# First attention: the scores of two heads computed together, with the high-times-high products in separate halves of the array's rows

## The chip, the cores and the metric

The kernel runs on one core of one Trainium2 chip, as one launch. The metric is the device time of that launch in microseconds. The time of a kernel is given as the median of several runs, and one further execution is recorded by the hardware profiler; its views (a page, groups of instructions by line, waits, the chain of waits, the order of time, sums by stretch) are what the text below reads. TensorE is called PE, its weight loads PEld, VectorE DVE, ScalarE ACT, GpSimd POOL and SyncE SP.

## The reference, cut to what matters

The program is a network of several layers on a sequence of 1024 positions of 256 values: a causal attention, a feed-forward part that selects positions, a second attention, the feed-forward part again, and a last layer with a recurrence. Only the first attention is touched:

```python
B, S, HID = (1, 256, 256)      # the hidden states that are given have S = 1024
H, KVH, HD = (32, 8, 64)
q = (hidden_states @ Wq.T).reshape(b, s, H, HD).transpose(0, 2, 1, 3)
k = (hidden_states @ Wk.T).reshape(b, s, KVH, HD).transpose(0, 2, 1, 3)
v = (hidden_states @ Wv.T).reshape(b, s, KVH, HD).transpose(0, 2, 1, 3)
...
q = apply_rope(q)
k = apply_rope(k)
k = jnp.repeat(k, groups, axis=1)          # groups = 4
v = jnp.repeat(v, groups, axis=1)
logits = jnp.einsum('bhqd,bhkd->bhqk', q, k) * scale
logits = jnp.where(causal, logits, jnp.finfo(dtype).min)
attn = jax.nn.softmax(logits, axis=-1)
out = jnp.einsum('bhqk,bhkd->bhqd', attn, v)
out = out.transpose(0, 2, 1, 3).reshape(b, s, H * HD)
return out @ Wo.T
```

So there are eight groups of four query heads that share one key head and one value head, of 64 values each, and a query sees the keys up to its own position.

## The kernel before

Positions are handled in eight tiles of 128 (`t` from 0 to 7), heads in eight groups (`g`, with `HG = 4` query heads each). A value is kept as two numbers of a format with fewer bits (F32R): a high part, which is the rounded value, and a low part, which is the rest. A product of two such values is the sum of up to four products of parts.

For each group and tile, `project` (L345 and after) multiplies by the weights, applies the rotation in DVE (L360 to L369), and makes the high and low parts of the four query heads and the one key head: a cast on ACT (L373) writes the high parts, and two subtractions write the low parts (the first group on DVE, all later ones on POOL, through the helper `pair`, L216). In the tile `qk` they lie as low, high for each head. `flip` transposes them on PE (L385 for queries, L392 for keys) and copies the results to `qs` and `ks` (ACT, L389 and L396). After that a head's low part is in rows 0 to 63 and its high part in rows 64 to 127 of `qs[:, h]`; `ks[:, 0]` holds the key as low over high, `ks[:, 1]` as high over low. One matmul over all 128 rows then gives two products of parts at once: with `ks[:, 0]` low times low plus high times high, with `ks[:, 1]` the two mixed ones.

For tile `t` there are `n = (t + 1) * 128` keys. `spans(n)` gives the number `k` of PSUM banks (1 up to 512 columns, otherwise 2) and the columns `w` in each. The scores of a head are made in one of two forms:

- for `t >= 4`, `scores` takes one head: two matmuls for each bank (L409), one more that adds the causal mask to the last 128 columns (L413), and then `softmax`: the maximum on DVE (L298), the exponential with its sum on ACT (L303), the reciprocal on DVE (L306) and the normalisation on POOL (L307);
- for `t < TWO`, with `TWO = 4`, `two_scores` takes two heads: each has one bank of the same tile `s`, with two matmuls and a mask matmul each (L428, L429), one reduce on DVE for both maxima (L430), two exponentials (L433), two reciprocals (L436) and two normalisations (L438).

A tile `s` has two banks, and there are two such tiles; all other matmul results of the stage use four further tiles `b` of one bank. After the scores, `turn` transposes the weights of four heads for one block of 128 keys (L444), `split_pt` makes their high part on ACT (L313) and their low part on DVE (L314), and `mix` multiplies them with the values (L455, L456). `fold` adds the two halves of the result (L466, L470, and POOL by L219 and L216), and `wout` multiplies by the output weights (L224 to L226) and adds to `x` (L484).

The order of the work is set by a list of events with due times, `(time, step)`, which is sorted and then issued. Its unit is one block of 128 keys, and a tile takes `n = t + 1 + GAP` units. The scores of tile `t` are due ahead of its first `turn`, by `LEAD` and a share of `A_LEN * n`; `PH` shifts the pairs. Each engine runs its instructions in the order that the scheduler of the program gives it from these events; an instruction that is ready may be placed between two of another event.

Of the kernel before, what the change touches and what calls it, by code (L numbers as in the profile page):

```python
# [10 lines left out]
F32 = mybir.dt.float32  # L11
# [4 lines left out]
AF = mybir.ActivationFunctionType  # L16
ALU = mybir.AluOpType
AX = mybir.AxisListType
PSUM = bass.MemoryType.PSUM

P = 128
T = 1024
# [11 lines left out]
LEAD = 4.56  # L34
# [21 lines left out]
A_LEN = 0.94  # L56
LAG = 2.22
GAP = 0.79
TWO = 4
PH = 0.62  # L60


def f(ap):
    return ap.bitcast(F32)
# [19 lines left out]
def spans(n):  # L84

    k = (n + 511) // 512
    return k, n // k


class Net:  # L90
# [227 lines left out]
    def attn_a(self):  # L318
        nc, tc = self.nc, self.tc
        G, HG, HD = 8, 4, 64  # L320
        NQ = HG + 1
        with ExitStack() as ctx:
            pool = self.layer_pool(ctx, "aa")
            grp = {}
# [19 lines left out]
            def project(g, t):  # L344
                z = grp[g]  # L345
                o = slice(t * P, t * P + P)
                pq = self.ps("b", bufs=4)
                for c in range(2):
                    self.mm3(
                        pq[:, : NQ * HD + HD], [a[c][:, o] for a in xT],  # L350
                        [a[:, c, :] for a in z["wq"]], c == 0, c == 1,
                    )
                raw = pool.tile([P, NQ + 1, HD], F32, tag="t1", name=self.nm("t1"))
                t2 = pool.tile([P, NQ, HD], F32, tag="t2", name=self.nm("t2"))
                p3 = pq[:, : NQ * HD + HD].rearrange("p (h d) -> p h d", d=HD)
                q3, t1 = p3[:, :NQ, :], raw[:, :NQ, :]
                cb = cos[:, t : t + 1, :].to_broadcast([P, NQ, HD])
                for a in range(2):
                    sb = sin[:, t : t + 1, 32 * a : 32 * a + 32].to_broadcast([P, NQ, 32])
                    nc.vector.tensor_tensor(  # L360
                        t2[:, :, 32 * a : 32 * a + 32], q3[:, :, 32 - 32 * a : 64 - 32 * a],
                        sb, op=ALU.mult,
                    )
                nc.vector.tensor_tensor(t1, q3, cb, op=ALU.mult)
                v = z["v"]
                pv = pq[:, NQ * HD : NQ * HD + HD]
                nc.scalar.copy(v[:, t, 0, :], pv)
                nc.vector.tensor_tensor(v[:, t, 1, :], pv, f(v[:, t, 0, :]), op=ALU.subtract)
                nc.vector.tensor_tensor(t1, t1, t2, op=ALU.add)  # L369

                qk = pool.tile([P, NQ * 2 + 1, HD], F32R, tag="qk", name=self.nm("qk"))
                lo, hi = (qk[:, : NQ * 2, :].rearrange("p (h a) d -> p h a d", a=2)[:, :, a, :] for a in range(2))
                nc.scalar.copy(hi, t1)  # L373
                sub = self.pair if g else nc.vector.tensor_tensor
                sub(lo, t1, f(hi), op=ALU.subtract)
                sub(qk[:, NQ * 2, :], t1[:, HG, :], f(hi[:, HG, :]), op=ALU.subtract)
                z["qh"][t] = qk

            def flip(g, t):
# [17 lines left out]
                    z["ks"][:, :, o], pt[:, : 2 * P].rearrange("p (h q) -> p h q", q=P)  # L397
                )

            def scores(g, t, h, pr):  # L400
                z = grp[g]
                qs, ks = z["qs"], z["ks"]
                o = slice(t * P, t * P + P)
                n = (t + 1) * P
                s = self.ps("s", [P, 2, 512])
                k, w = spans(n)
                for b in range(k):
                    for a in range(2):
                        nc.tensor.matmul(  # L409
                            s[:, b, :w], qs[:, h, o], ks[:, a, b * w : (b + 1) * w],  # L410
                            start=a == 0, stop=a == 1 and b < k - 1,
                        )
                nc.tensor.matmul(s[:, k - 1, w - P : w], self.identb, self.maskb, start=False, stop=True)  # L413
                pr[h] = self.softmax(pool, 8, s[:, :k, :w], n)

            def two_scores(g, t, h0, pr):

                z = grp[g]
                qs, ks = z["qs"], z["ks"]
                o = slice(t * P, t * P + P)  # L420
                n = (t + 1) * P
                s = self.ps("s", [P, 2, 512])
                m, l, r = (
                    self.small.tile([P, 2], F32, tag=k, name=self.nm(k), bufs=6) for k in ("smm", "sml", "smr")
                )
                for i in range(2):
                    for a in range(2):
                        nc.tensor.matmul(s[:, i, :n], qs[:, h0 + i, o], ks[:, a, :n], start=a == 0, stop=False)  # L428
                    nc.tensor.matmul(s[:, i, n - P : n], self.identb, self.maskb, start=False, stop=True)  # L429
                nc.vector.tensor_reduce(m, s[:, :, :n], AX.X, ALU.max, negate=True)  # L430
                pp = [pool.tile([P, 512], F32, tag="p_", name=self.nm("p_"), bufs=8) for _ in range(2)]
                for i in range(2):
                    nc.scalar.activation(  # L433
                        pp[i][:, :n], s[:, i, :n], AF.Exp, bias=m[:, i : i + 1], scale=1.0, accum_out=l[:, i : i + 1]
                    )
                    nc.vector.reciprocal(r[:, i : i + 1], l[:, i : i + 1])  # L436
                for i in range(2):
                    nc.gpsimd.tensor_scalar(pp[i][:, :n], pp[i][:, :n], r[:, i : i + 1], 1.0, op0=ALU.mult, op1=ALU.mult)  # L438
                    pr[h0 + i] = pp[i]

            def turn(g, t, kt, pr, st):
                pt = self.ps("b", bufs=4)
                for h in range(HG):
                    nc.tensor.transpose(  # L444
                        pt[:, h * P : (h + 1) * P], pr[h][:, kt * P : (kt + 1) * P], self.ident,
                    )
                st[kt] = self.split_pt(pt, 512)

            def mix(g, t, kt, st):
                z = grp[g]  # L450
                if kt == 0:
                    st["po"] = self.ps("b", bufs=4)
                hi, lo = st.pop(kt)
                vv = z["v"][:, kt, :, :].rearrange("p a d -> p (a d)")
                nc.tensor.matmul(st["po"], vv, hi, start=kt == 0, stop=False)  # L455
                nc.tensor.matmul(st["po"], vv, lo, start=False, stop=kt == t)  # L456
# [29 lines left out]
            ev, at = [], 0.0  # L486
            for g in range(G):
                g0 = at
                for t in ORD[min(g, 1) + (g == G - 1)]:
                    n = t + 1 + GAP  # L490
                    pr, st = {}, {}
                    if t < TWO:
                        for h in range(0, HG, 2):
                            ev.append((at - LEAD - A_LEN * n + A_LEN * n * (h + PH) / HG, lambda g=g, t=t, h=h, pr=pr: two_scores(g, t, h, pr)))
                    for h in range(HG if t >= TWO else 0):
                        ev.append((at - LEAD - A_LEN * n + A_LEN * n * (h + 0.5) / HG, lambda g=g, t=t, h=h, pr=pr: scores(g, t, h, pr)))
                    for kt in range(t + 1):
                        ev.append((at + kt, lambda g=g, t=t, kt=kt, pr=pr, st=st: turn(g, t, kt, pr, st)))
                        ev.append((at + kt + LAG, lambda g=g, t=t, kt=kt, st=st: mix(g, t, kt, st)))
                    ev.append((at + t + LAG + 0.1, lambda g=g, t=t, st=st: fold(g, t, st)))  # L500
                    ev.append((at + t + LAG + 4, lambda g=g, t=t: wout(g, t)))
                    at += n
                if g + 1 < G:
                    d = at - g0
                    lo, hi = (g0 + w * d for w in ((W0, W1) if g else FIRST))
                    ev.append((lo, lambda g=g + 1: weights(g)))
                    for t in range(NT):
                        ev.append((lo + (hi - lo) * (t + 1) / NT, lambda g=g + 1, t=t: project(g, t)))
                        ev.append((lo + (hi - lo) * (t + 2.2) / NT, lambda g=g + 1, t=t: flip(g, t)))
            for t in range(NT):  # L510
                ev.append((PRO[0] + PRO[1] * t, lambda t=t: project(0, t)))
                ev.append((PRO[0] + PRO[1] * (t + PRO[2]), lambda t=t: flip(0, t)))
# [1152 lines left out]
```

## Time and profile before

| | |
|---|---|
| median of 3 runs | 1554.46 us (1554.23 to 1555.32) |
| the profiled execution | 1553.83 us |
| its span, from the first to the last instruction | 1552.1 us |
| mean granted TensorE clock over the span | 0.956 |
| PE, recorded busy | 1381.5 us (89%) |
| DVE | 1200.5 us (77%) |
| ACT | 945.3 us (61%) |
| POOL | 707.2 us (46%) |

The score matmuls of the first attention (L409, L428) run between about 30 and 630 us of the span. Matmul records have a start that is measured and an end that is modelled, so consecutive matmuls overlap in the records, and the distance between two starts tells what one costs. A group line gives the line, engine, operation, names, shapes and count, then the busy time in us and the mean of one in ns, then the engine's idle time before these instructions and what ended most of it. A line of the order of time gives the start in us, the length in us, the engine, the instruction and how many were merged.

### The profile page before, as it was taken

The page shows a single profiled execution, that of the slowest core. Times are in us where ns is not written, and L with a number is a line of the kernel's source. Part 1 is how long each engine was busy: PE and PEld are TensorE (multiplying, and loading weights), DVE is VectorE, ACT ScalarE, POOL GpSimd, SP SyncE. Part 2 cuts the span into 40 slices and gives each one's busy share as a digit, 9 for nine tenths or more (in the row PEclk, how much of TensorE's full clock was granted, in tenths as well). Part 3 has the DMA queues.
Part 4 walks back from the last instruction along what each step waited for, and adds up shares of the span by engine and source line. Part 5 has one row for each costly group of instructions (what it writes and reads, how often), then busy time and mean ns, then how long its engine had stood idle before and what let it go on. Part 6 is the DMA issues. An engine that isn't in the chain of part 4 may idle for free. (4 is left out here: it accounts for less than half of the span.)

```text
span 1552.1 us, 25113 instructions
## 1 busy us (share of the span) xinstructions
PE 1381.5 (89%) x8626; PEld 1143.4 (74%) x8626; DVE 1200.5 (77%) x2562; ACT 945.3 (61%) x2049; POOL 707.2 (46%) x1059
## 2 busy tenths in 40 slices
PE   5999999999999999677789999999996786986898
PEld 4788888888888888546678788877885464765787
DVE  5888999999998999864667777775774666977657
ACT  4777777777878787622466665665563432555533
POOL 4656666666565654523654534544312322346100
PEclk9999999999999999899899999999998697997999
DMA  3000000000000020330265555555568311000000
GB/s 95 11 8 11 8 11 8 12 8 12 8 1 1 1 82 29 113 109 21 47 119 106 112 113 109 115 101 109 89 138 233 143 58 37 28 21 1 1 1 28
DMA packets 169391, 87.65 MB, mean 56 GB/s; under 512 B 154032, under 2 KB 154288, under 8 KB 166960
## 3 DMA queue, kind: packets, MB, share of 16 engines
q1 hardware_dynamic: 169264, 86.05, 23.0%
q8 instruction: 68, 1.11, 0.3%
q14 instruction: 59, 0.48, 0.1%
HBM read 47.23 MB, written 1.05 MB: 31 GB/s over the span
## 5 line engine op out<-in xcount | busy, mean ns | idle before, releaser
L314 DVE TENSOR_TENSOR pt<-b,pt 128x512 fp32r<-128x512 f32 x288 | 192.8, 684 | 22.4 <-ACT pt L313 18.8
L313 ACT CAST pt<-b 128x512 fp32r<-128x512 f32 x288 | 165.1, 591 | 46.6 <-PE b L444 43.5
L307 POOL TENSOR_SCALAR p<-p,smr 128x640 f32<-128x640 f32 (+3 forms) x128 | 125.5, 980 | 89.9 <-DVE smr L306 82.7
L303 ACT ACTIVATE p<-s,smm 128x640 f32<-128x640 f32 (+3 forms) x128 | 123.2, 963 | 25.9 <-DVE smm L298 21.2
L298 DVE TENSOR_REDUCE smm<-s 128x1 f32<-128x640 f32 (+3 forms) x128 | 129.7, 1013 | 5.6 <-PE s L413 5.2
L409 PE MATMUL s<-ks,qs 128*128 128x320 f32 (+3 forms) x512 | 133.3, 366 | 0.6 <-ACT p L303 0.5
L455 PE MATMUL b<-pt,v 128*128 128x512 f32 x288 | 132.5, 460 | 0.3 <-ACT pt L313 0.3
L444 PE MATMUL b<-ident,p 128*128 128x128 f32 x832 | 122.8, 273 | 0.2 <-ACT qs L389 0.2
L456 PE MATMUL b<-pt,v 128*128 128x512 f32 x288 | 120.6, 419 | 0.1
L444 PEld LDWEIGHTS b<-ident,p 128*128 128x128 f32 x832 | 96.9, 141 | 10.7 <-ACT qs L389 1.8
L409 PEld LDWEIGHTS s<-ks,qs 128*128 128x128 f32 x512 | 89.3, 189 | 13.0 <-ACT p L303 4.2
L734 PE MATMUL b<-ptr,v 128*128 128x256 f16 (+1 forms) x320 | 83.4, 266 | 10.7 <-DMA ptr<-hl 9.4
L678 ACT ACTIVATE p<-s,smm 128x640 f32<-128x640 f32 (+1 forms) x64 | 60.8, 950 | 47.9 <-DVE smm L676 47.7
L216 POOL TENSOR_TENSOR qk<-t,qk 128x320 fp32r<-128x320 f32 x112 | 64.5, 597 | 49.9 <-ACT qk L373 49.9
L667 PE MATMUL s<-qk 128*128 128x320 f32 (+3 forms) x384 | 85.7, 358 | 0.5 <-ACT p L678 0.3
L735 PE MATMUL b<-ptr,v 128*128 128x256 f16 (+1 forms) x320 | 84.8, 265 | 0.0
L716 DVE SCALAR_TENSOR_TENSOR hl<-p,smr,hl 128x640 f16<-128x640 f32 (+1 forms) x64 | 71.7, 1120 | 15.2 <-ACT hl L701 13.6
L736 PE MATMUL b<-ptr,v 128*128 128x256 f16 (+1 forms) x320 | 83.3, 265 | 0.0
L701 ACT ACTIVATE hl<-p,smr 128x640 f16<-128x640 f32 (+1 forms) x64 | 63.2, 988 | 19.8 <-DVE smr L695 11.7
L693 POOL TENSOR_SCALAR p<-p,smr 128x128 f32<-128x128 f32 (+1 forms) x64 | 33.7, 532 | 88.4 <-DVE smr L691 81.5
L428 PE MATMUL s<-ks,qs 128*128 128x256 f32 (+3 forms) x256 | 66.9, 356 | 4.5 <-ACT p__78_391 L433 1.7
L667 PEld LDWEIGHTS s<-qk 128*128 128x128 f32 x384 | 65.4, 188 | 7.5 <-ACT p L678 1.4
(1036 smaller groups left out, 4554.5 us busy)
## 6 DMA issues: line engine op xcount, KB each, us to landing
wqkv<-in_wqkv_f SPq DMA_DIRECT2D x8, 1024.0 KB, 5.9
wof<-in_wo_f SPq DMA_DIRECT2D x4, 1024.0 KB, 6.8
bias<-in_bqkv_f SPq DMA_DIRECT2D x16, 256.0 KB, 3.4
raw<-in_wqk_b SPq DMA_DIRECT2D x16, 256.0 KB, 3.3
wgu<-in_wgu_f SPq DMA_DIRECT2D x4, 1024.0 KB, 6.1
raw<-in_wqkv_a SPq DMA_DIRECT2D x8, 384.0 KB, 3.2
raw<-in_wo_a SPq DMA_DIRECT2D x8, 256.0 KB, 2.7
wd<-in_wd_f SPq DMA_DIRECT2D x2, 1024.0 KB, 4.7
```

The lines of the kernel that those rows point to most:

```text
L298: nc.vector.tensor_reduce(m, s, AX.XY, ALU.max, negate=True)
L303: nc.scalar.activation(p[:, :n].rearrange("p (a b) -> p a b", a=s.shape[1]), s, AF.Exp, bias=m, scale=1.0, accum_out=l)
L307: nc.gpsimd.tensor_scalar(p[:, :n], p[:, :n], r, 1.0, op0=ALU.mult, op1=ALU.mult)
L313: nc.scalar.copy(hi[:, :n], pt[:, :n])
L314: nc.vector.tensor_tensor(lo[:, :n], pt[:, :n], f(hi[:, :n]), op=ALU.subtract)
L409: nc.tensor.matmul(s[:, b, :w], qs[:, h, o], ks[:, a, b * w : (b + 1) * w], start=a == 0, stop=a == 1 and b < k - 1,)
L444: nc.tensor.transpose(pt[:, h * P : (h + 1) * P], pr[h][:, kt * P : (kt + 1) * P], self.ident,)
L455: nc.tensor.matmul(st["po"], vv, hi, start=kt == 0, stop=False)
L456: nc.tensor.matmul(st["po"], vv, lo, start=False, stop=kt == t)
L667: nc.tensor.matmul(s[:, i, :w], z[a][:, o], z[b][:, i * w : (i + 1) * w], start=j == 0, stop=j == 2 and i < k - 1,)
L734: nc.tensor.matmul(d, vh, hi, start=kt + i == 2 * b, stop=False)
L735: nc.tensor.matmul(d, vh, lo, start=False, stop=False)
```

## The change

`scores` and `two_scores` become one function that handles two heads for every tile. The queries of the second head of each pair are stored as high over low, those of the first as low over high. The two mixed products of a head remain one matmul over all rows, with the key copy that fits. Low times low is no longer computed. High times high is a matmul over 64 rows: for the first head rows 64 to 127, for the second rows 0 to 63, each into a bank of its own. All mixed products of the pair come first, then the halves, then the two masks. For `t >= 4` the pair takes both tiles `s`. The maximum is reduced for each head by itself in every tile. The high parts are cast by two instructions on ACT, one for the queries and one for the key, and the low part of the key is written twice by one subtraction. The due times of the tiles with `t >= 4` are now those of pairs.

```diff
--- before.py
+++ after.py
@@ -56,7 +56,6 @@
 A_LEN = 0.94
 LAG = 2.22
 GAP = 0.79
-TWO = 4
 PH = 0.62
 
 
@@ -369,11 +368,14 @@
                 nc.vector.tensor_tensor(t1, t1, t2, op=ALU.add)
 
                 qk = pool.tile([P, NQ * 2 + 1, HD], F32R, tag="qk", name=self.nm("qk"))
-                lo, hi = (qk[:, : NQ * 2, :].rearrange("p (h a) d -> p h a d", a=2)[:, :, a, :] for a in range(2))
-                nc.scalar.copy(hi, t1)
+                q4, tq = qk[:, : 2 * HG, :].rearrange("p (j a) d -> p j a d", a=4), t1[:, :HG, :].rearrange("p (j e) d -> p j e d", e=2)
+                hi, lo = q4[:, :, 1:3, :], q4[:, :, 0:4:3, :]
+                hik, lok = qk[:, 2 * HG + 1 : 2 * HG + 2, :], qk[:, 2 * HG : 2 * HG + 3 : 2, :]
+                nc.scalar.copy(hi, tq)
+                nc.scalar.copy(hik, t1[:, HG:NQ, :])
                 sub = self.pair if g else nc.vector.tensor_tensor
-                sub(lo, t1, f(hi), op=ALU.subtract)
-                sub(qk[:, NQ * 2, :], t1[:, HG, :], f(hi[:, HG, :]), op=ALU.subtract)
+                sub(lo, tq, f(hi), op=ALU.subtract)
+                sub(lok, t1[:, HG:NQ, :].to_broadcast([P, 2, HD]), f(hik).to_broadcast([P, 2, HD]), op=ALU.subtract)
                 z["qh"][t] = qk
 
             def flip(g, t):
@@ -397,46 +399,49 @@
                     z["ks"][:, :, o], pt[:, : 2 * P].rearrange("p (h q) -> p h q", q=P)
                 )
 
-            def scores(g, t, h, pr):
+            def scores(g, t, h0, pr):
+
+
                 z = grp[g]
                 qs, ks = z["qs"], z["ks"]
                 o = slice(t * P, t * P + P)
                 n = (t + 1) * P
-                s = self.ps("s", [P, 2, 512])
                 k, w = spans(n)
+                s = [self.ps("s", [P, 2, 512]) for _ in range(k)]
+                s = [s[i] for i in range(2)] if k == 2 else [s[0][:, i : i + 1, :] for i in range(2)]
+                for i in range(2):
+                    for b in range(k):
+                        nc.tensor.matmul(
+                            s[i][:, b, :w], qs[:, h0 + i, o], ks[:, 1 - i, b * w : (b + 1) * w], start=True, stop=False,
+                        )
                 for b in range(k):
-                    for a in range(2):
+                    for i in range(2):
+                        half = slice(64 * (1 - i), 64 * (1 - i) + 64)
                         nc.tensor.matmul(
-                            s[:, b, :w], qs[:, h, o], ks[:, a, b * w : (b + 1) * w],
-                            start=a == 0, stop=a == 1 and b < k - 1,
+                            s[i][:, b, :w], qs[half, h0 + i, o], ks[half, i, b * w : (b + 1) * w],
+                            start=False, stop=b < k - 1,
                         )
-                nc.tensor.matmul(s[:, k - 1, w - P : w], self.identb, self.maskb, start=False, stop=True)
-                pr[h] = self.softmax(pool, 8, s[:, :k, :w], n)
-
-            def two_scores(g, t, h0, pr):
-
-                z = grp[g]
-                qs, ks = z["qs"], z["ks"]
-                o = slice(t * P, t * P + P)
-                n = (t + 1) * P
-                s = self.ps("s", [P, 2, 512])
+                for i in range(2):
+                    nc.tensor.matmul(s[i][:, k - 1, w - P : w], self.identb, self.maskb, start=False, stop=True)
                 m, l, r = (
-                    self.small.tile([P, 2], F32, tag=k, name=self.nm(k), bufs=6) for k in ("smm", "sml", "smr")
+                    self.small.tile([P, 2], F32, tag=k_, name=self.nm(k_), bufs=6) for k_ in ("smm", "sml", "smr")
                 )
                 for i in range(2):
-                    for a in range(2):
-                        nc.tensor.matmul(s[:, i, :n], qs[:, h0 + i, o], ks[:, a, :n], start=a == 0, stop=False)
-                    nc.tensor.matmul(s[:, i, n - P : n], self.identb, self.maskb, start=False, stop=True)
-                nc.vector.tensor_reduce(m, s[:, :, :n], AX.X, ALU.max, negate=True)
-                pp = [pool.tile([P, 512], F32, tag="p_", name=self.nm("p_"), bufs=8) for _ in range(2)]
+                    c = slice(i, i + 1)
+                    nc.vector.tensor_reduce(m[:, c], s[i][:, :, :w], AX.XY, ALU.max, negate=True)
+                    if n > 512:
+                        p = self.get("P", [P, T], F32, "p")
+                    else:
+                        p = pool.tile([P, 512], F32, tag="p_", name=self.nm("p_"), bufs=8)
+                    nc.scalar.activation(
+                        p[:, :n].rearrange("p (a b) -> p a b", a=k), s[i][:, :, :w], AF.Exp, bias=m[:, c], scale=1.0,
+                        accum_out=l[:, c],
+                    )
+                    nc.vector.reciprocal(r[:, c], l[:, c])
+                    pr[h0 + i] = p
                 for i in range(2):
-                    nc.scalar.activation(
-                        pp[i][:, :n], s[:, i, :n], AF.Exp, bias=m[:, i : i + 1], scale=1.0, accum_out=l[:, i : i + 1]
-                    )
-                    nc.vector.reciprocal(r[:, i : i + 1], l[:, i : i + 1])
-                for i in range(2):
-                    nc.gpsimd.tensor_scalar(pp[i][:, :n], pp[i][:, :n], r[:, i : i + 1], 1.0, op0=ALU.mult, op1=ALU.mult)
-                    pr[h0 + i] = pp[i]
+                    p = pr[h0 + i][:, :n]
+                    nc.gpsimd.tensor_scalar(p, p, r[:, i : i + 1], 1.0, op0=ALU.mult, op1=ALU.mult)
 
             def turn(g, t, kt, pr, st):
                 pt = self.ps("b", bufs=4)
@@ -489,11 +494,8 @@
                 for t in ORD[min(g, 1) + (g == G - 1)]:
                     n = t + 1 + GAP
                     pr, st = {}, {}
-                    if t < TWO:
-                        for h in range(0, HG, 2):
-                            ev.append((at - LEAD - A_LEN * n + A_LEN * n * (h + PH) / HG, lambda g=g, t=t, h=h, pr=pr: two_scores(g, t, h, pr)))
-                    for h in range(HG if t >= TWO else 0):
-                        ev.append((at - LEAD - A_LEN * n + A_LEN * n * (h + 0.5) / HG, lambda g=g, t=t, h=h, pr=pr: scores(g, t, h, pr)))
+                    for h in range(0, HG, 2):
+                        ev.append((at - LEAD - A_LEN * n + A_LEN * n * (h + PH) / HG, lambda g=g, t=t, h=h, pr=pr: scores(g, t, h, pr)))
                     for kt in range(t + 1):
                         ev.append((at + kt, lambda g=g, t=t, kt=kt, pr=pr, st=st: turn(g, t, kt, pr, st)))
                         ev.append((at + kt + LAG, lambda g=g, t=t, kt=kt, st=st: mix(g, t, kt, st)))
```

## The prediction

> **What bounds the kernel now.** First the busy digits of the page, to find the stretch that the change touches, then the sums of that stretch by engine.
>
> ```profile
> PE   5999999999999999677789999999996786986898
> DVE  5888999999998999864667777775774666977657
> ```
> ```profile
> core 0: us, PE busy (x) PEld busy (x) DVE busy (x) ACT busy (x) POOL busy (x), PEclk, DMA share, GB/s
> 60.00:600.00 540.00, 535.19 (x3467) 451.04 (x3467) 489.72 (x1100) 422.84 (x983) 329.15 (x494) 1.00 0.04 14
> ```
>
> The first attention fills slices 2 to 16 (about 40 to 640 us). PE is recorded busy for 535.19 of 540 us, DVE for 489.72, at full clock and with hardly any DMA. The chain that ended last is followed back only to the second half of the span, so it says nothing here; and recorded matmul ends are modelled, so PE must be read by its starts. The order of time of PE alone gives those:
>
> ```profile
> 230.65 0.34 PE L226 MATMUL b<-wh,xT 128*128 128x384 f32 x1
> 230.83 0.33 PE L224 MATMUL b<-wh,xT 128*128 128x384 f32 x1
> 231.00 0.33 PE L225 MATMUL b<-wl,xT 128*128 128x384 f32 x1
> ...
> 232.36 0.44 PE L409 MATMUL s<-ks,qs 128*128 128x384 f32 x1
> 232.64 0.38 PE L392 MATMUL b<-ident,qk 128*128 128x128 f32 x2
> 232.78 0.59 PE L409 MATMUL s<-ks,qs 128*128 128x384 f32 x2
> ...
> 234.76 0.23 PE L413 MATMUL s<-maskb,identb 128*128 128x128 bf16 x1
> 234.80 0.47 PE L455 MATMUL b<-pt,v 128*128 128x512 f32 x1
> 235.12 0.39 PE L456 MATMUL b<-pt,v 128*128 128x512 f32 x1
> 235.34 0.40 PE L455 MATMUL b<-pt,v 128*128 128x512 f32 x1
> 235.58 0.46 PE L409 MATMUL s<-ks,qs 128*128 128x320 f32 x2
> ```
>
> Four things are seen. A 384-column matmul starts 0.17 us after the last, but is recorded with 0.33 to 0.34: some 0.163 us of each is a tail that the next one overlaps. After a mask matmul, which the next follows by 0.04 us, a 512-column matmul costs 0.32 (234.80 to 235.12) where it otherwise costs 0.22 to 0.24: its weight load, recorded at 188 ns, is then not hidden, for about 85 ns. A chain of scores is not kept together: at 232.64 the transposes of L392 stand inside one. And there are few holes. Over all starts from 60 to 600 us I count about 480 to 500 us of such starts' own distances, 33 us of 85 ns load exposures (400 of them) and some 20 us of longer holes. So PE bounds this stretch, with about 4% to spare; DVE comes next with 9% (50 us of 540) idle. What PE gains can be used only until DVE binds, at about half its size; what PE loses is paid nearly in full.
>
> **The change part by part.** Start distances within the chains of L409 are 146, 175, 202 and 231 ns for 320, 384, 448 and 512 columns (t = 4 to 7); 256 columns of L224 to L226 take 118.
>
> Matmuls removed. Per pair of heads and bank, four full products become two full and two half-row ones. If the two halves run beside each other, one start distance goes. Nothing in the trace runs two matmuls at once. Bounds: no gain (halves one after the other), or a whole distance: for t = 0 to 7 109, 118, 175, 231, then twice 146, 175, 202 and 231, 2141 ns; 16 pairs of each t (8 groups by 2), 34.3 us. I take less, since each half has a weight load of its own, and 128-column transposes, whose loads are as many as they, come every 109 ns: two halves then cost the larger of one distance and 220 ns. Saved: 0, 18, 130, 231, 144, 260, 368, 462 = 1613 ns by 16 = **25.8 us**.
>
> Masks. Both masks of a pair now stand at its end: one 85 ns exposure of a following load instead of two, but the second mask's own load (recorded at 96 ns) shows beyond the 38 ns of the first, about 58. Saved 27 ns by 128 pairs = **3.5 us** (0 to 10.9).
>
> Changes of the array's partition. Each pair goes from 128 rows to two halves and back: 256 changes. In the count of starts, 70 of 496 L409 matmuls (14%) have a foreign one next. With three borders inside a pair's halves for t of 4 and more and one below (256 borders), 14% broken adds two changes each, 72: **328 in all**. No matmul of the trace uses fewer than 128 rows, so the price has to be bounded: 0 (nothing is waited for), or the tail and a whole unhidden load, 163 + 188 = 351 ns. Below nothing is excluded, for a change does no work. I take the tail alone, 163 ns, the row nearest to waiting until the array is empty: 328 × 0.163 = **53.5 us**. The weights are loaded ahead everywhere in this trace, so I leave their 188 ns to the range.
> The row first: the 0.163 us tail is overlapped at every start shown, full array after full array. The Trainium skill, "TensorEngine Tiling (Array Packing)", Key Properties, states a rule that speaks against this change: going to another tiling mode, not just another tile, drains the engine. By it each of the 328 changes pays, without it none, and the sum would be 29 us of PE saved; no row here can show which.
> For the overlap of the halves, the nearest row is the 231 ns between 512-column starts. The skill's "TensorE: Matmul & The Clock Gate", Part 3, has row tiles start about 4 ns apart; by that page the saving would be the upper bound of 34.3 us, and it says nothing of tiles that alternate with the full array.
>
> DVE. For t below 4 one reduce of both heads becomes two. From the rows:
>
> ```profile
> L298 DVE TENSOR_REDUCE smm<-s 128x1 f32<-128x1024 f32 x32 | 38.8, 1213 | 1.9 <-PE s L413 1.7
> L298 DVE TENSOR_REDUCE smm<-s 128x1 f32<-128x640 f32 x32 | 26.0, 813 | 0.3 <-PE s L413 0.2
> L430 DVE TENSOR_REDUCE smm<-s 128x2 f32<-128x256 f32 x16 | 6.6, 411 | 0.0
> ```
>
> (1213 − 813) / 384 = 1.042 ns per element, so 146 ns are fixed; 64 more reduces add 9.3 us. DVE's 50 idle us hide it as long as PE binds: 0, and up to 9.3 if not.
>
> ACT and POOL. The 320-column cast of L373 (462 ns) becomes 256 columns (408 by the 128x256 cast of L875) and 64 (222 by L367): +168 ns, 64 times, 10.8 us on an engine with 117 of 540 idle: 0. POOL's two subtractions keep their total (872 + 321 ns against about 736 + 459). Who waits behind:
>
> ```profile
> POOL qk L216 <- ACT qk L373: 49.9, 24, 3.4
> ...
> PEld s L409 <- ACT p L303: 4.0, 16, 0.5
> ```
>
> POOL waits longer for that cast, but PE waited for POOL's result only 1.7 us in all; without that cover 10.8 us. No DMA is added, and nothing moves on SP's queue.
>
> Buffers. For t of 4 and more a pair now takes both score buffers at once, and the next pair's first matmul, with all transposes and mixes queued behind it on PE, waits for the first exponential of this one. Pairs come 0.47 n units apart; 8 groups of 42.3 units in about 595 us make a unit 1.76 us, so 7.3 us for t = 7 and 4.8 for t = 4. The buffer is held for matmuls, two reduces and an exponential, about 1.6 + 2.4 + 1.3 + 0.4 = 5.7 and 1.0 + 1.6 + 1.0 + 0.4 = 4.0 us. It fits: 0, taken from the second row above (4.0 us of waits today); if it does not, about 0.5 us by 64 pairs, 32 us.
>
> Sum on PE: − 25.8 − 3.5 + 53.5 = **+24.2 us**, paid in full. The profiled execution took 1553.83 us (span 1552.1 and 1.7 around it), 0.6 below the median of the runs, so 1553.8 + 24.2 + 0.6 = 1578.6: **1578 us**.
>
> **The rivals.**
> *The changes are cheap* (0 to 50 ns). For it: PE reorders nothing but hides every load here. Against: the tail must go somewhere. PE then saves 29 down to 13 us; half can be used before DVE binds, and the 9.3 us of reduces take some back: 1540 to 1552, say **1545**. It decides below 29.3 / 328 = 89 ns per change: beneath that the kernel is not slower.
> *Load not hidden either*, 351 ns: 328 × 0.351 = 115 − 29 = +86; some changes share their wait, so 250 ns and more, 1607 to 1640, say **1620**. For it: after a mask the load is already exposed by 85 ns.
> *The halves run one after the other*, so the change does not do what it says: 53.5 − 3.5 = +50 us, **1604**. For it: no two matmuls overlap in the trace.
> *The buffers do not suffice*: with the forecast's price +24 + 32, **1610**; with cheap changes + 32 − 10, 1576.
>
> **How the numbers follow.** Forecast (tail alone, 1564 to 1592) 0.32; cheap changes 0.31; load exposed 0.17; halves in turn 0.11; buffers 0.09. The likeliest is 1578. The range goes from 1543, which leaves out the better part of the cheap case (about 0.1), to 1618, which leaves out the dearest load cases (0.1). About 0.2% (3.1 us) is what a measurement can tell from no change. Faster: 0.27, nearly all of the cheap case; same 0.05, from its upper end; slower 0.68.
>
> **What would show it.** Right: half-row score matmuls of which two start closer together than 100 ns, the gap from the last full matmul to the first half at 0.16 us or more beyond its usual distance, and again on the way back to the masks; the stretch of the first attention some 24 us longer, all later stretches the same; DVE's idle share in it higher than 9%. Wrong: starts that follow without a gap at the change (the cheap case), halves a whole distance apart, more than 20 us of PE waiting for ACT at the scores (buffers), or DVE's idle time nearly gone with PE showing holes (DVE the bound).

## The result, and the profile after

The changed kernel takes 1605.77 us (median of 4 runs) where the kernel before takes 1554.89 us in the same series: a ratio of 1.0338, with a 95% interval of 1.0310 to 1.0365. It is slower by 51 us. The forecast was 24 us slower: the direction and the range hold, the size does not. The profiled execution took 1604.71 us, with a span of 1602.8 us.

The busy digits of the page after (PE, then DVE), to be held against those of before: the first attention now reaches about a slice further.

```profile
PE   5999999999999999977589999999897676886898
DVE  6888888888888888876467677767774767887666
```

The sums over the stage, from 20 us to its end, for the kernel before (620 us) and after (676 us). The columns are the stretch, its length, then busy time and number of instructions of PE, PEld, DVE, ACT and POOL, the clock, the DMA share and GB/s.

```profile
20.00:640.00 620.00, 605.42 (x3897) 509.18 (x3896) 556.76 (x1279) 482.58 (x1134) 365.66 (x555) 0.99 0.05 18
```
```profile
20.00:696.00 676.00, 649.96 (x3900) 491.14 (x3898) 565.07 (x1346) 491.98 (x1199) 365.95 (x556) 1.00 0.05 16
```

DVE and ACT work some 8 and 9 us more, POOL the same; DVE's idle share goes from 10% to 16%. PE's recorded time grows although its products became fewer. What it grows by is seen in the order of time of PE after (start, length, instruction; L414 full products, L420 halves, L425 masks):

```profile
291.59 0.64 PE L414 MATMUL s<-ks,qs 128*128 128x512 f32 x2
292.16 0.73 PE L420 MATMUL s<-ks,qs 64*128 64x512 f32 x2
292.82 0.23 PE L425 MATMUL s<-maskb,identb 128*128 128x128 bf16 x1
...
309.74 0.48 PE L414 MATMUL s<-ks,qs 128*128 128x256 f32 x2
310.15 0.39 PE L420 MATMUL s<-ks,qs 64*128 64x256 f32 x2
310.47 0.29 PE L425 MATMUL s<-maskb,identb 128*128 128x128 bf16 x2
...
338.11 0.30 PE L414 MATMUL s<-ks,qs 128*128 128x320 f32 x1
338.35 0.56 PE L420 MATMUL s<-ks,qs 64*128 64x320 f32 x3
338.83 0.44 PE L394 MATMUL b<-ident,qk 128*128 128x128 f32 x2
...
340.35 0.41 PE L420 MATMUL s<-ks,qs 64*128 64x320 f32 x1
340.69 0.29 PE L425 MATMUL s<-maskb,identb 128*128 128x128 bf16 x2
```

Three readings. At 310.15 two halves last 0.39 us together: they start 4 ns apart, and the mask behind them starts 0.32 us after the first, where a half of 256 columns that stands alone (in the run with single halves below) is followed after 0.31. So they do run beside each other. The Trainium skill ("TensorE: Matmul & The Clock Gate", Part 3) has about 4 ns between row tiles, and this trace agrees. At 292.16 two halves of 512 columns last 0.73 us: they follow each other. There the order of the program has one head alone, its two banks in the same half of the rows, with one mask behind them. And at 338.35 the first half starts 0.24 us after a full product of 320 columns, whose own distance is 0.146: the array is first emptied, for about 0.09 us. A first half is recorded with 0.41 us against 0.30 for a later one: its load starts with it and is not hidden, 0.107 us more. On the way out (340.35 to 340.69) one half costs 0.34 us: 0.107 for its load, 0.146 of its own, 0.09 to empty. So going into halves and out again costs some 0.28 us, more if the next full product's load also shows. Over all 207 ways in the median excess is 93 ns, over the 207 ways out 186. The rule of the Trainium skill ("TensorEngine Tiling (Array Packing)", Key Properties) that a change of mode drains the engine holds here; the unhidden load comes on top of it.

The page's group lines of the weight loads of the score products, before (L409) and after (L420), say the same: loads are as long as ever, but the load path stands idle before those of the halves, with nothing that it waits for in the profile.

```profile
L409 PEld LDWEIGHTS s<-ks,qs 128*128 128x128 f32 x512 | 89.3, 189 | 13.0 <-ACT p L303 4.2
```
```profile
L420 PEld LDWEIGHTS s<-ks,qs 64*128 64x128 f32 x384 | 48.2, 184 | 50.4 <-issue 47.4
```

From all starts of PE, from 20 us to the last product with the values, I count where its time goes. A product's own distance is its columns at 2.4 per ns and 17 ns more (109 for a transpose, 38 for a mask, nothing for a half that another follows within 20 ns), or the measured distance where that is smaller; what goes beyond is put down by what comes next. All in us:

| | before | after | pairs, all rows | same half | kept together | single halves |
|---|---|---|---|---|---|---|
| score products, own distances | 134.9 | 122.3 | 134.9 | 135.7 | 104.4 | 135.9 |
| beyond, at changes of partition | 0 | 50.6 (414) | 0 | 44.9 (414) | 36.8 (290) | 132.8 (768) |
| beyond, between halves (the first one's load) | 0 | 9.7 | 0 | 17.2 | 7.2 | 0 |
| other excess below 130 ns | 58.2 | 53.6 | 58.1 | 53.4 | 54.6 | 40.9 |
| holes of 130 ns and more | 26.8 | 41.0 | 52.5 | 40.4 | 85.0 | 17.0 |
| halves beside another | – | 86 | – | 0 | 175 | 0 |
| end of the stage | 638.0 | 693.9 | 660.7 | 708.6 | 707.1 | 743.4 |

After against before: − 12.6 + 50.6 + 9.7 − 4.6 + 14.2 (and − 1.6 on other products and masks) make up, but for rounding, the 55.9 us by which the stage ends later. Of the 86 halves beside another, 63 belong to the 64 pairs for t below 4, whose two heads share one buffer, and only 23 to the 128 possible ones for t of 4 and more. The rest of the span is 5 us shorter (50.7 in all), in code that was not changed; why is not settled. The columns to the right belong to the experiments.

### The profile page after: what moved, and what is told of

Read it like the earlier page. It is cut to its first block, busy times and chain, and to the rows that moved or that the text cites. A ratio compares the mean times of both kernels' runs of the same rounds, so it can differ in the third digit from the quotient of the medians.

```text
span 1602.8 us, 25250 instructions
## 1 busy us (share of the span) xinstructions
PE 1425.0 (89%) x8626; PEld 1125.3 (70%) x8626; DVE 1205.2 (75%) x2626; ACT 954.0 (60%) x2113; POOL 706.7 (44%) x1059
## 5 line engine op out<-in xcount | busy, mean ns | idle before, releaser
L431 DVE TENSOR_REDUCE smm<-s 128x1 f32<-128x512 f32 (+7 forms) x256 | 188.1, 748 | 34.9 <-PE s L425 33.2
L461 PE MATMUL b<-pt,v 128*128 128x512 f32 x288 | 122.3, 425 | 0.0
L414 PE MATMUL s<-ks,qs 128*128 128x512 f32 (+5 forms) x384 | 115.6, 370 | 4.7 <-ACT p L436 2.3
L420 PE MATMUL s<-ks,qs 64*128 64x512 f32 (+5 forms) x384 | 108.7, 413 | 0.0
L449 PEld LDWEIGHTS b<-ident,p 128*128 128x128 f32 x832 | 96.4, 141 | 13.4 <-ACT p L436 1.2
L215 POOL TENSOR_TENSOR qk<-t,qk 128x256 fp32r<-128x256 f32 x112 | 64.3, 595 | 79.2 <-ACT qk L374 79.2
L420 PEld LDWEIGHTS s<-ks,qs 64*128 64x128 f32 x384 | 48.2, 184 | 50.4 <-issue 47.4
L414 PEld LDWEIGHTS s<-ks,qs 128*128 128x128 f32 x384 | 64.2, 189 | 23.9 <-ACT p L436 11.4
```

Of the source, the lines that this page charges most:

```text
L414: nc.tensor.matmul(s[i][:, b, :w], qs[:, h0 + i, o], ks[:, 1 - i, b * w : (b + 1) * w], start=True, stop=False,)
L420: nc.tensor.matmul(s[i][:, b, :w], qs[half, h0 + i, o], ks[half, i, b * w : (b + 1) * w], start=False, stop=b < k - 1,)
L431: nc.vector.tensor_reduce(m[:, c], s[i][:, :, :w], AX.XY, ALU.max, negate=True)
L449: nc.tensor.transpose(pt[:, h * P : (h + 1) * P], pr[h][:, kt * P : (kt + 1) * P], self.ident,)
```

## The experiments

Medians of before differ between series (1552.7 to 1556.1 us), so kernels are compared by their ratio to before in the same series, with its 95% interval.

**Is it the divided array? Pairs with all rows.** The order of PE's instructions is that of the changed kernel, product for product.

```diff
-                        half = slice(64 * (1 - i), 64 * (1 - i) + 64)
+                        half = slice(0, 128)
```

> The changed kernel, with its third and fourth products of a pair taken over all 128 rows instead of 64 (high times high then carries low times low along, as in the kernel before). Pairs, buffers, casts, reduces and the order of all instructions stay those of the changed kernel; only the array is never divided. Theory A (changes of the array's partition are what costs): the changed kernel's trace has 414 changes with 50.6 us beyond the matmuls' own distances, and 9.7 us between halves that follow each other; both go, and the overlap of the halves (about 13 us) is lost: 1606 - 60 + 13 = about 1559 us, at most 1570. Theory B (a pair that takes both score buffers, the extra reduces and casts are what costs): nothing of that is undone, so 1590 us or more.

Measured: 1578.91 us, ratio 1.0156 (1.0128 to 1.0185). Neither theory alone: by the ratios (1.0338 and 1.0156) about 28 us go with the divided array, and some 24 stay without it. In the table the excess at changes is gone, the products cost what they did before, and the holes are 52.5 us against 26.8.

**Is the overlap worth anything?**

```diff
-                        half = slice(64 * (1 - i), 64 * (1 - i) + 64)
+                        half = slice(64, 128)
```

> The changed kernel, with both heads' 64-row products in rows 64 to 127, so that no two can run beside each other (the second head's product is then not the one that is wanted). Order and number of instructions are unchanged, and so is the number of changes of partition. If the overlap of the halves is worth what the trace says: about 86 to 110 pairs of halves that start 3 to 4 ns apart now start one own distance plus some 0.1 us apart: + 20 to 30 us, 1626 to 1636 us. If PE does not bind any more in the changed kernel, or the overlap is worth nothing: 1603 to 1610 us.

Measured: 1620.41 us, 1.0417 (1.0390 to 1.0444), some 12 us above the changed kernel by the ratios (15 by the medians). This is less than the 20 to 30 that were expected, but not nothing: by the table PE's products, halves and changes cost 15 us more, and most of that is paid in time. A stretch of its PE shows what two halves in the same rows do:

```profile
338.41 0.60 PE L414 MATMUL s<-ks,qs 128*128 128x384 f32 x2
338.93 0.61 PE L420 MATMUL s<-ks,qs 64*128 64x384 f32 x2
339.48 0.28 PE L425 MATMUL s<-maskb,identb 128*128 128x128 bf16 x2
```

The two halves now last 0.61 us, where two of 384 columns that overlap last 0.44 in the changed kernel.

**The price of a change by itself.** Scores by single heads, buffers and due times as before, new layout, and after each full product its own half:

```diff
+                        rows = slice(64 * (1 - i), 64 * (1 - i) + 64) if a else slice(0, 128)
-                            s[:, b, :w], qs[:, h, o], ks[:, a, b * w : (b + 1) * w],
+                            s[:, b, :w], qs[rows, h, o], ks[rows, i if a else 1 - i, b * w : (b + 1) * w],
```

> The scores by single heads and buffers as before, on the new layout, with high times high over 64 rows directly behind each full product (no two halves can overlap, and no buffer is needed earlier). In program order each of the 384 products of a head and bank is entered and left by itself: about 768 changes of the array's partition. Theory A (a change costs 0.12 to 0.145 us wherever it stands): 92 to 111 us above the run with the layout alone, near 1655 us. Rival (changes are cheap, and the lost time of the changed kernel comes from its order): within 20 us of it.

Measured: 1663.49 us, 1.0701 (1.0669 to 1.0734), 97 us above the layout alone (1566.19): 0.127 us of time per change for the 768 changes. PE's starts hold 132.8 us of excess at them (0.173 each); the holes and the other excess shrink by 39 against those of the layout alone (36.7 and 60.4). In its profile four products of one head, two full and two half, last 1.66 us, where four full ones of 448 columns follow each other by 0.2 us:

```profile
332.68 1.66 PE L414 MATMUL s<-ks,qs 128*128 128x448 f32 x4
334.27 0.23 PE L418 MATMUL s<-maskb,identb 128*128 128x128 bf16 x1
```

**Keeping the four halves of a pair together.**

```diff
+                        with tc.issue_after(last.ins):      # last: the pair's last full product
                             nc.tensor.matmul(
```

> The changed kernel, with every 64-row product ordered behind the last full product of its pair, so that the four halves of a pair stand together. By the order of the program: 145 entries into halves instead of 207, and 177 of 192 halves of two heads next to each other instead of 39. Theory A: 124 changes fewer at about 0.145 us are 18 us, and some 90 more overlaps with their loads another 20 to 27 us: 1560 to 1575 us. Theory B: PE now waits longer for the second score buffer: 1600 us or more, with the wait of PE for ACT at the scores above 20 us from 60 to 600 us.

Measured: 1620.46 us, 1.0421 (1.0395 to 1.0446): a miss for theory A. Overlaps rise from 86 to 175 and changes fall to 290, as meant; products and changes cost 34 us less than in the changed kernel, though with 148 us still 13 more than the 135 of the pairs with all rows. (The 39 neighbours that the expectation counts for the changed kernel are not what its trace has: 86 overlap there.) Here four halves of 512 columns, two beside two, last as long as the two at 292.16 in the changed kernel:

```profile
205.74 0.73 PE L421 MATMUL s<-ks,qs 64*128 64x512 f32 x4
206.40 0.29 PE L426 MATMUL s<-maskb,identb 128*128 128x128 bf16 x2
```

But the holes double, to 85.0 us. The waits from 60 to 600 us (who, for whom, us in total, times, longest) name the cause, the second score buffer; the changed kernel has 8.5 and 1.4 us in these lines.

```profile
PEld s L414 <- ACT p L437: 40.1, 53, 1.5
...
PE s L414 <- ACT p L437: 22.8, 33, 1.2
```

So for t of 4 and more a pair can have its overlap only by waiting for both buffers; where it does not wait, the order of the program issues the heads one after the other, and the overlap is lost. That the missing second buffer is what splits them is inferred from this run and from the 63 of 64 where one buffer is enough; the scheduler itself was not looked into.

**The change for t below 4 alone.**

> The change for the tiles t below 4 alone (pairs that share one buffer, as before); the tiles of 4 and more have the scores of the kernel before, on the new layout. By the order of the program 82 entries into halves. Theory A: 164 changes at 0.145 us are 24 us, saved matmuls 16 x 0.58 = 9 us, so 12 to 18 us slower than before: 1567 to 1573 us. Theory B: no pair takes two buffers, so 1555 to 1560 us.

The edit: pairs with halves in place of `two_scores`, the other scores as before on the new layout. Measured: 1576.08 us, 1.0138 (1.0114 to 1.0163), 10 us above the layout alone and somewhat more than theory A gave. Its 64 pairs share one buffer, and 63 halves do overlap; PE's own score time falls by 9.3 us, as expected, but 130 changes cost 19.3. Where the overlap works as meant, it still costs more than it saves.

**The layout alone, and the split reduce alone.** They are the casts and subtractions of the change with before's scores, and this edit:

```diff
-                nc.vector.tensor_reduce(m, s[:, :, :n], AX.X, ALU.max, negate=True)
+                for i in range(2):
+                    nc.vector.tensor_reduce(m[:, i : i + 1], s[:, i, :n], AX.X, ALU.max, negate=True)
```

> The kernel before, with the changed kernel's layout of the high and low parts alone: two casts on ACT and the other two subtractions; the scores run as before, one head at a time for t of 4 and more, all rows. Theory A (casts hidden, as predicted): 1551 to 1558 us. Theory C (the longer way from rotation to transposes over ACT and POOL reaches PE): 1563 to 1572 us, a third or more of the 25 us by which the changed kernel without a divided array was slower than before.

> The kernel before, with one reduce for each head in the tiles t below 4 instead of one for both; nothing else. As predicted (9.3 us more on DVE, hidden while PE binds): 1553 to 1556 us. If DVE's added work is paid: 1560 to 1564 us.

Measured: 1566.19 us, 1.0073 (1.0049 to 1.0097), and 1557.68 us, 1.0027 (1.0011 to 1.0042). The layout, forecast at nothing, costs 11 us; the reduce about 4 of its 9.3.

**What in the layout costs?** Four kernels: the cast cut in two on the old layout; the layout with the key's cast on DVE; the layout with one cast over six slots; and the kernel before with a cast that nobody reads:

```diff
                 nc.scalar.copy(hi, t1)
+                side = pool.tile([P, 1, HD], F32R, tag="side", name=self.nm("side"))
+                nc.scalar.copy(side, t1[:, HG:NQ, :])
```

> The kernel before, old layout, with the cast of the high parts on ACT cut in two (four query heads, one key head) and nothing else: the 10.8 us of ACT time that the prediction took as hidden. If ACT's second cast is what the layout costs: 1563 to 1568 us, as the run with the layout alone (1566). If it is hidden, and the layout's cost lies in the subtractions or in the order: 1553 to 1557 us.

> The layout alone, with the key's high part cast on DVE in place of ACT. If the load of ACT is the cause: 1553 to 1560 us. If it is the second step in the chain to the transposes, or the new order, whatever engine does it: 1562 us or more.

> The layout alone, with one cast on ACT for all high parts: it takes six slots of 64 (the sixth holds a product that is not used; its low neighbour is overwritten by the key's second low part), so that the rotation's multiplication grows by 64 columns on DVE and the second cast is gone. If the second step of the cast is what the layout costs: 1554 to 1560 us. If it is the other subtractions or the new order: 1564 us or more.

> The kernel before, with one more cast of 64 columns on ACT for each group and tile into a tile that nobody reads; the chain to the transposes keeps its single cast. If the time of an extra instruction (by load, or by the order that it leads to) is what counts: 1563 to 1570 us. If it must stand in the chain to the transposes: 1553 to 1558 us.

Measured: 1569.54 us, 1.0088 (1.0069 to 1.0107); 1567.68, 1.0077 (1.0058 to 1.0097); 1569.77, 1.0105 (1.0083 to 1.0128); 1566.62, 1.0082 (1.0059 to 1.0105). The second cast is enough for the cost; it may stand on DVE; and it need not be read by anyone. That is against a longer chain to the transposes. One cast of six slots does not mend it, so the number of casts is not the point either: it adds a little work to DVE and loses as much. The group lines of the dead cast and of its neighbour, the part of `split_pt` on ACT:

```profile
L313 ACT CAST pt<-b 128x512 fp32r<-128x512 f32 x288 | 165.7, 590 | 64.3 <-PE b L446 54.0 <-DVE x L486 8.3 <-DVE pt L314 0.7
...
L375 ACT CAST side<-t 128x64 fp32r<-128x64 f32 x64 | 15.9, 248 | 0.0
```

It is 15.9 us of ACT, and about 13 us of time, on an engine that was idle for 137 of 620 us.

**Or is it the order?** Small changes of before's due times add no work, but change the order of all instructions. The last kernel has the dead cast and another lead.

```diff
-LEAD = 4.56
+LEAD = 4.66
```
```diff
-A_LEN = 0.94
+A_LEN = 0.97
```
```diff
-LAG = 2.22
+LAG = 2.32
```

> The kernel before with LEAD at 4.66 in place of 4.56: no instruction is added or removed, the scores are due a tenth of a unit (0.18 us) earlier, and the program's order changes. It gives the size of what a new order alone does. If the order matters little: within 2 us of before. If differences of 10 us can come from the order alone: 1558 us or more.

> The kernel before with A_LEN 0.97 in place of 0.94: no work added, other due times for the scores, hence another order. If an order of its own can cost what a small extra step costs (about 12 us): 1562 us or more. If it needs the extra work: 1552 to 1559 us.

> The kernel before with LAG 2.32 in place of 2.22: no work added, products with the values, folds and output products due a tenth of a unit later. If an order of its own can cost about 12 us: 1562 us or more. If it needs the extra work: 1552 to 1559 us.

> The kernel before with the cast that nobody reads (1567), and LEAD at 4.66. The work is that of e_side_cast in yet another order. If the 12 us are the work itself: 1564 to 1570 us again. If they are the order: anything else, 1562 us or less among it.

Measured: 1559.91 us, 1.0020 (1.0001 to 1.0040); 1558.38, 1.0021 (1.0005 to 1.0036); 1557.69, 1.0017 (0.9998 to 1.0035); and with the dead cast 1563.65, 1.0053 (1.0038 to 1.0068). Three other orders cost about 3 us each, hardly more than the intervals can tell from nothing; the extra cast costs 8 and 13 us in the two orders tried. This points to the small piece of work itself for the larger part, but does not prove it: each order was one try, and none was found in which the cast is free. By which wait it reaches PE was not shown, nor whether due times chosen anew for the changed kernel would win some of it back.

**What do the pairs for t of 4 and more cost?** Three kernels, all rows, t below 4 as before, on the new layout: pairs as in the change; single heads due at the pairs' times; and pairs with the first head's products and mask all ahead of the second's.

```diff
-                for b in range(k):                       # full products of both heads come first,
-                    for i in range(2):                   # then these, then both masks
+                for i in range(2):                       # all of one head, then all of the other
+                    for b in range(k):
```

> Layout and pairs for t of 4 and more as in the changed kernel, but all rows in every product; the tiles t below 4 stay with their two heads in one buffer and one reduce. Theory B (a pair that takes both score buffers costs): 12 to 25 us above the run with the layout alone. Rival (the buffers suffice, and the 25 us are the casts and the reduces): within 4 us of the run with the layout alone.

> The layout alone, with the single heads' scores for t of 4 and more due at the times of the pairs; each head still takes a buffer only for itself. If the 13.7 us between the layout alone and the pairs over all rows are the due times: 1576 to 1583 us. If they are the buffers taken together: 1563 to 1569 us.

> The pairs over all rows for t of 4 and more (1580), with the first head's five matmuls all ahead of the second's, so that its mask, reduce and exponential are not held back. If the pair costs because the first head's scores are finished late: 1566 to 1572 us, near the single heads at the pairs' due times (1570). If taking both buffers together costs: 1576 us or more.

Measured: 1579.86 us, 1.0168 (1.0139 to 1.0198); 1570.24, 1.0094 (1.0071 to 1.0117); 1567.87, 1.0093 (1.0065 to 1.0120). The pairs cost 15 us above the layout alone; the due times are about 3 of it. With the first head's products and mask in front, the pair costs no more than the due times do. So it is the order inside the pair that costs some 12 us. That order changes two things at once: the first head's mask, and with it its reduce and exponential, waits until the second head is nearly done, and PE needs the second buffer earlier. These runs do not separate the two. The waits from 60 to 600 us, for the pairs with all rows for t of 4 and more (first fence) and for those with the first head in front (second), show more of PE waiting for buffers than of DVE waiting for the pairs' masks:

```profile
PEld s L456 <- ACT p L478: 7.6, 17, 0.9
PEld s L431 <- ACT p L478: 7.0, 16, 0.7
DVE smm L473 <- PE s L467: 3.5, 8, 1.8
```
```profile
PEld s L457 <- ACT p L472: 3.2, 7, 0.5
DVE smm L467 <- PE s L461: 6.0, 18, 0.4
```

Over all lines of this kind, PEld and PE wait 20.4 and 5.3 us for exponentials at the scores in the first, 8.0 and 0.9 in the second; a first head that is finished late also frees its buffer late. In the changed kernel, where t below 4 has such pairs too, DVE's wait for the masks is the larger one:

```profile
DVE smm L431 <- PE s L425: 27.3, 48, 1.1
```

No kernel here beats the one before.

## Why the prediction was right in direction and wrong in size

**What bounds the stage.** Right in the main, but what PE loses is not paid nearly in full. Taking the overlap away costs PE 15 us and the kernel about 12; 133 us of excess at changes cost 97; and the 48 us that the divided array costs PE in the changed kernel (60.3 less the 12.6 saved) are worth 28.

**Changes of partition.** Forecast 53.5 us from 328 changes at 0.163. Measured 60.3 us (50.6 and 9.7) at 414, 0.146 each. The price, taken from the tail alone, was near by luck, for it is made of other parts: about 0.09 us each way to empty the array and a load of 0.107, which the forecast had left to its range. Its own sign, a gap of 0.16 us or more before the first half, is not seen; the gap is 0.09. The count was too low, since pairs for t of 4 and more are issued head by head.

**Matmuls saved.** Forecast 25.8 us, measured 12.6: this term is half its size. It took all 192 pairs of halves as overlapping; 86 do. This is the first step that failed, and it rests on the one on the buffers, which found that they suffice and priced a lack of them as PE waiting. PEld and PE waited little for them (13.4 and 2.9 us from 60 to 600 us, 7.1 and 1.9 before); instead the order split the pairs for t of 4 and more. The loads of two halves beside each other did not set a floor of 220 ns.

**Masks.** Forecast − 3.5 us, and the short excess fell by 4.6; no run took it by itself.

**What was put at nothing.** The casts, the reduce and the order inside a pair were costed at 0, because ACT and DVE had idle time and PE had waited only 1.7 us for POOL. Alone they cost 11, 4 and about 12 us, and some 24 together in the pairs with all rows. This is the second step that failed, and about half of the error: idle shares were taken as cover, and in the changed kernel PE has 14 us more of holes. That they appear smaller there is probably because a slower PE gives the other engines more time; the parts do not add. By which waits the small steps reach PE stays open.

**The sum.** Forecast on PE − 25.8 − 3.5 + 53.5 = 24.2. By the same terms measured: − 12.6 − 4.6 + 60.3 = 43, and 14 of holes, less 1.6 and the 5 that came back after the stage: 51. The result lies inside the range only because that was drawn wide for dearer loads, which is not what happened.

**The rivals.** Cheap changes are out (single halves: 0.127 us each against a turning point of 0.089). An unhidden load at every change, at 0.351, is out as a price; on the way in it is there. Halves one after the other is half true: 106 of 192. Buffers that do not suffice seem to have shown as split pairs; as the wait that this rival named they showed only where the halves were kept together.

## What to carry to other kernels

A half-row product must save more than the way into halves and out costs: here 0.28 us, more than one full product of 512 columns (0.23), so several halves have to share one way in. In the kernel that keeps them together, the median for four halves of 512 columns is 0.76 us with the way in and out, where four full products at their usual distance take 0.92; two halves take 0.53 against 0.46, and four of 320 columns save nothing (0.585 against 0.584). A kernel that divides the array only for the widest tiles, with buffers enough, was not tried. Two products overlap only if nothing comes between them in the order that is actually issued; where they need two buffers at once, count how often both are free. And the idle share of an engine is no cover: in a stage where PE, DVE and ACT feed each other, 16 us of work on an engine idle for a fifth of the time came with 8 to 13 us, so a small added step is better priced at most of its own length than at nothing.

## What was not expected of the hardware

Loads of 189 ns are hidden behind full products that follow each other by 146 to 231 ns, but the first load for a half starts only with the half, about 0.09 us after the full product before it is through: the load path stood idle for 50.4 us before 384 loads. Two halves beside each other cost no more than one: from the first start to the next product 259 ns at 128 columns and 430 at 512 (medians of the changed kernel), where a half alone takes 256 and 429 (run with single halves). So their two loads of 184 ns did not add up.
